# Seven-product form for every 512-cubed product of a two-layer graph network, and layer 1's weights as row dot products

## The chip, the cores and the metric

The kernel runs on one core of one Trainium2 chip. The metric is the device time of one execution in microseconds (us), less is better. All runs quoted of one kernel agree within about 0.3%. TensorE multiplies matrices, VectorE, ScalarE and GpSimd work element by element, and each engine takes its instructions in one fixed order. In the profile they are PE (PEld is its weight load), DVE, ACT and POOL.

## The reference, cut to what matters

There are 32 independent batches of 512 nodes with 512 features, all in f32. LN is a LayerNorm without parameters.

```
h  = max(LN(x), 0)
x  = x + relu([h, (adj h) / deg] W^T)          # layer 0, deg = row sums of adj
h1 = max(LN(x), 0)
q, k = split(h1 Wqk);  v = h1 Wv               # layer 1
w  = scale * mask * rowsum(q * (adj (mask k)))
x  = x + softmax(w)[:, None] * v
```

Both kernels fold Wq Wk^T into one 512x512 matrix once, so k is never formed. Per batch six products of 512 cubed are left.

## The kernel before

Each product is taken in four row chunks of 128. A chunk adds four matmuls of a 128x128 stationary block and 512 columns in one bank of PSUM:

```python
def product(p, pairs):
    for i, (lhsT, rhs) in enumerate(pairs):
        nc.tensor.matmul(p, lhsT, rhs, start=(i == 0), stop=(i == len(pairs) - 1))
```

LayerNorm's scaling runs on VectorE, and its relu is taken when ScalarE copies the transposed chunk out of PSUM. Layer 1's weights come from the full 512x512 matrix of q times h1, multiplied by the masked adj while its rows are summed. Four buffers each of x and adj let the loads run far ahead.

```python
def transpose_block(dst, src, c, func, name):
    p = ps_t.tile([P, 4, P], F32, tag="t", name=name)
    for d in range(4):
        nc.tensor.transpose(p[:, d, :], src[:, ts(d, P)], ident)
    nc.scalar.activation(dst[:, :, ts(c, P)], p, func)
# ... in layer1(b), after q^T = (h1 m)^T:
for c in range(C):
    p = mm_tile(f"ps_{b}_{c}")
    product(p, [(q[:, e, ts(c, P)], h1T[:, e, :]) for e in range(D)])
    nc.vector.scalar_tensor_tensor(
        am[:, c, :], p, mcol[:, c, b:b + 1], am[:, c, :],
        op0=ALU.mult, op1=ALU.mult, accum_out=w[:, c:c + 1])
# ...
for i in range(B + 1):   # layer 0 of batch i, layer 1 of i - 1, preparation of i + 1
    ...
```

The source gives a program order. The framework's scheduler turns it, by durations that it estimates, into one fixed instruction order for each engine; a later instruction is put ahead where an earlier one is thought not to be ready.

Of the kernel before, what the change touches and what calls it, by code (L numbers as in the profile page):

```python
# [15 lines left out]
P = 128  # L16
DEG_EPS = 1e-6
# [4 lines left out]
def kernel(  # L22
# [10 lines left out]
    """Layer 0: x1 = x + relu([h | adj h / deg] W^T), h = relu(LN(x)).  # L33
    Layer 1: out = x1 + softmax_i(w) * (h1 Wv), h1 = relu(LN(x1)), with
    w_i = scale m_i sum_j adj_ij m_j (q_i . k_j) and q_i . k_j = h1_i (Wq Wk^T) h1_j.

    Both layers use h only with the features on the partitions, so LN's result is
    transposed and the relu is taken on the way out of PSUM. adj / deg goes through
    the transpose already scaled, so that both halves of layer 0 add up in one
    PSUM bank as h W1^T + (adj / deg) (h W2^T).  # L40
    """
    nc = tc.nc
# [8 lines left out]
    small = ctx.enter_context(tc.tile_pool(name="small", bufs=4))  # L51
    ps_t = ctx.enter_context(tc.tile_pool(name="ps_t", bufs=2, space=bass.MemoryType.PSUM))
    ps_m = ctx.enter_context(tc.tile_pool(name="ps_m", bufs=5, space=bass.MemoryType.PSUM))
    ps_s = ctx.enter_context(tc.tile_pool(name="ps_s", bufs=1, space=bass.MemoryType.PSUM))

    def tile4(tag, bufs, name):
        return big.tile([P, 4, 512], F32, tag=tag, bufs=bufs, name=name)

    X, A, MB = {}, {}, {}

    def load(b):
        X[b] = tile4("x", 4, f"x_{b}")
        nc.sync.dma_start(out=X[b], in_=x[b].rearrange("(c p) f -> p c f", p=P))
        A[b] = tile4("adj", 4, f"adj_{b}")
        nc.sync.dma_start(out=A[b], in_=adj[b].rearrange("(c p) j -> p c j", p=P))
        MB[b] = small.tile([P, N], F32, tag="mb", name=f"mb_{b}")
        nc.sync.dma_start(out=MB[b], in_=nodemask[b].partition_broadcast(P))

    def transpose_block(dst, src, c, func, name):
        """dst[:, d, block c] = func(src[:, d-th block]^T) for the 4 blocks d of src [P, 512]."""  # L70
        p = ps_t.tile([P, 4, P], F32, tag="t", name=name)
        for d in range(4):
            nc.tensor.transpose(p[:, d, :], src[:, ts(d, P)], ident)  # L73
        nc.scalar.activation(dst[:, :, ts(c, P)], p, func)  # L74

    def product(p, pairs):
        for i, (lhsT, rhs) in enumerate(pairs):
            nc.tensor.matmul(p, lhsT, rhs, start=(i == 0), stop=(i == len(pairs) - 1))  # L78

    def mm_tile(name):  # L80
        return ps_m.tile([P, 512], F32, tag="m", name=name)

# [9 lines left out]
    wv_sb = const.tile([P, D, F], F32, name="wv_sb")  # L92
    mask_sb = const.tile([B, N], F32, name="mask_sb")
    w_in = []
    for half, tag in ((w0[:, 0:F], "x"), (w0[:, F:2 * F], "x"), (wqk[:, 0:F], "adj"), (wqk[:, F:2 * F], "adj")):
        t = tile4(tag, 4, f"w_in{len(w_in)}")
        nc.sync.dma_start(out=t, in_=half.rearrange("(c p) f -> p c f", p=P))
        w_in.append(t)
    nc.sync.dma_start(out=wv_sb, in_=wv.rearrange("(c p) f -> p c f", p=P))
    nc.sync.dma_start(out=mask_sb, in_=nodemask)  # L100
    load(1)

    w1T = const.tile([P, D, F], F32, name="w1T")
    w2T = const.tile([P, D, F], F32, name="w2T")
    wqT = tile4("q", 1, "wqT")
    wkT = tile4("h1T", 1, "wkT")
    m_sb = const.tile([P, D, F], F32, name="m_sb")

    XN, HT, AT = {}, {}, {}

    def layer_norm(b, name):
        """(x - mean) / sqrt(var + eps) of X[b], row chunk by row chunk."""
        mv = small.tile([P, C, 2], F32, tag="mv", name=f"mv{name}")
        rstd = small.tile([P, C], F32, tag="rstd", name=f"rstd{name}")
        for c in range(C):
            st = small.tile([P, 6], F32, tag="st", name=f"st{name}_{c}")
            nc.vector.bn_stats(st, X[b][:, c, :])  # L117
            nc.vector.bn_aggr(mv[:, c, :], st)
        nc.vector.tensor_scalar(rstd, mv[:, :, 1], LN_EPS, None, op0=ALU.add)  # L119
        nc.gpsimd.tensor_tensor(rstd, rstd, mhalf, op=ALU.pow)  # L120
        xn = tile4("xn", 2, f"xn{name}")
        for c in range(C):
            nc.vector.tensor_scalar(  # L123
                xn[:, c, :], X[b][:, c, :], mv[:, c, 0:1], rstd[:, c:c + 1],
                op0=ALU.subtract, op1=ALU.mult,
            )
        return xn

    def prepare(b):
        xn = layer_norm(b, f"0_{b}")  # L130
        rdeg = small.tile([P, C], F32, tag="rdeg", name=f"rdeg_{b}")
        nc.vector.tensor_reduce(rdeg, A[b], AX.X, ALU.add)
        nc.vector.tensor_scalar(rdeg, rdeg, DEG_EPS, None, op0=ALU.max)
        nc.vector.reciprocal(rdeg, rdeg)
        an = tile4("an", 1, f"an_{b}")
        for c in range(C):
            nc.vector.tensor_scalar(an[:, c, :], A[b][:, c, :], rdeg[:, c:c + 1], None, op0=ALU.mult)  # L137
        HT[b] = tile4("hT", 2, f"hT_{b}")
        for c in range(C):
            transpose_block(HT[b], xn[:, c, :], c, AF.Relu, f"pth_{b}_{c}")  # L140
        AT[b] = tile4("aT", 2, f"aT_{b}")
        for c in range(C):
            transpose_block(AT[b], an[:, c, :], c, AF.Copy, f"pta_{b}_{c}")
        mb = MB.pop(b)
        for c in range(C):
            nc.gpsimd.tensor_tensor(A[b][:, c, :], A[b][:, c, :], mb, op=ALU.mult)  # L146

    def layer0_y(b):
        y = tile4("y", 1, f"y_{b}")
        for c in range(C):  # L150
            p = mm_tile(f"py_{b}_{c}")
            product(p, [(HT[b][:, d, ts(c, P)], w2T[:, d, :]) for d in range(D)])
            nc.scalar.activation(y[:, c, :], p, AF.Copy)  # L153
        return y

    def layer0_out(b, y):
        hT, aT = HT.pop(b), AT.pop(b)
        for c in range(C):
            p = mm_tile(f"po_{b}_{c}")
            product(  # L160
                p,
                [(hT[:, d, ts(c, P)], w1T[:, d, :]) for d in range(D)]
                + [(aT[:, j, ts(c, P)], y[:, j, :]) for j in range(C)],
            )
            nc.vector.scalar_tensor_tensor(  # L165
                X[b][:, c, :], p, 0.0, X[b][:, c, :], op0=ALU.max, op1=ALU.add
            )
        XN[b] = layer_norm(b, f"1_{b}")

    def layer1_h(b):  # L170
        h1T = tile4("h1T", 1, f"h1T_{b}")
        xn = XN.pop(b)
        for c in range(C):
            transpose_block(h1T, xn[:, c, :], c, AF.Relu, f"pt1_{b}_{c}")
        return h1T

    def layer1(b, h1T):
        q = tile4("q", 1, f"q_{b}")
        for e in range(D):
            p = mm_tile(f"pq_{b}_{e}")  # L180
            product(p, [(m_sb[:, d, ts(e, P)], h1T[:, d, :]) for d in range(D)])
            nc.scalar.activation(q[:, e, :], p, AF.Copy)  # L182

        pv = {}

        def v_chunk(c):
            pv[c] = mm_tile(f"pv_{b}_{c}")
            product(pv[c], [(h1T[:, d, ts(c, P)], wv_sb[:, d, :]) for d in range(D)])

        v_chunk(0)  # L190
        am = A.pop(b)
        w = small.tile([P, C], F32, tag="w", name=f"w_{b}")
        for c in range(C):
            p = mm_tile(f"ps_{b}_{c}")
            product(p, [(q[:, e, ts(c, P)], h1T[:, e, :]) for e in range(D)])
            nc.vector.scalar_tensor_tensor(  # L196
                am[:, c, :], p, mcol[:, c, b:b + 1], am[:, c, :],
                op0=ALU.mult, op1=ALU.mult, accum_out=w[:, c:c + 1],
            )
        top = small.tile([P, 1], F32, tag="top", name=f"top_{b}")  # L200
        nc.vector.tensor_reduce(top, w, AX.X, ALU.max)
        v_chunk(1)
        ptop = ps_s.tile([1, P], F32, tag="s", name=f"ptop_{b}")
# [3 lines left out]
        v_chunk(2)  # L207
        pbc = ps_s.tile([P, 1], F32, tag="s", name=f"pbc_{b}")
# [7 lines left out]
        v_chunk(3)  # L216
        psum = ps_s.tile([P, 1], F32, tag="s", name=f"psum_{b}")
# [3 lines left out]
        sm = small.tile([P, C], F32, tag="sm", name=f"sm_{b}")  # L221
        nc.vector.tensor_scalar(sm, e, rs, None, op0=ALU.mult)
        xo = X.pop(b)
        for c in range(C):
            nc.vector.scalar_tensor_tensor(
                xo[:, c, :], pv[c], sm[:, c:c + 1], xo[:, c, :], op0=ALU.mult, op1=ALU.add
            )
        nc.sync.dma_start(out=out[b].rearrange("(c p) f -> p c f", p=P), in_=xo)

# [1 line left out]
    prepare(0)  # L231
    for t, dst in zip(w_in, (w1T, w2T, wqT, wkT)):
        for c in range(4):
            transpose_block(dst, t[:, c, :], c, AF.Copy, f"ptw_{dst.name}_{c}")
    for d in range(D):
        p = mm_tile(f"pm_{d}")
        product(p, [(wqT[:, a, ts(d, P)], wkT[:, a, :]) for a in range(D)])
# [47 lines left out]
```

## Time and profile before

| | before |
|---|---|
| median of the runs | 2885.6 us |
| span of the profiled run | 2883.9 us |
| TensorE busy | 2860 us, 99% |
| next busiest engine | VectorE, 29% |
| one batch, steady | 88.45 us |

TensorE's busy share is an upper view of its work, because matmul records overlap. The distance from one matmul's start to the next one's is the better measure. The prediction below shows these lines.

### The profile page before, as it was taken

The numbers are of one execution on the slowest core, as the hardware profiler recorded it, in microseconds if no ns is written. First come the engines' busy times: TensorE is split into PE (matmuls) and PEld (weight loads), VectorE is DVE, ScalarE is ACT, GpSimd is POOL, SyncE is SP. The second block draws the span as 40 slices with busy tenths as digits, with TensorE's granted clock in tenths as the row PEclk, the third lists the DMA queues.
The fourth block names the chain that finished last, engine by engine and source line by source line (L and its number), as shares of the span: only waits on it lengthen the run. The fifth ranks groups of instructions, "written<-read, shape, count | busy, mean of one in ns | idle before, by whom it ended". The sixth has DMA issues, their size and how long they took to land.

```text
span 2883.9 us, 19045 instructions
## 1 busy us (share of the span) xinstructions
PE 2860.2 (99%) x7940; PEld 1356.2 (47%) x7940; DVE 837.3 (29%) x1762; ACT 381.5 (13%) x694; POOL 240.6 (8%) x198
## 2 busy tenths in 40 slices
PE   8999999999999999999999999999999999999998
PEld 4444444444444444444444444444444444444443
DVE  4323323233232232232332323322323323232111
ACT  3111011111011110111100111101111011111000
POOL 2101011010010110110100101101001011010000
PEclk9999999999999999999999999999999999999999
DMA  5011001110011110011100111100111001110000
GB/s 216 4 48 48 15 33 48 48 48 30 29 36 47 48 48 15 33 48 48 47 30 19 48 48 47 46 17 33 48 48 48 15 29 44 44 44 15 0 15 29
DMA packets 58070, 115.58 MB, mean 40 GB/s; under 512 B 2144, under 2 KB 2144, under 8 KB 57984
## 3 DMA queue, kind: packets, MB, share of 16 engines
q1 hardware_dynamic: 57984, 114.37, 11.4%
q8 instruction: 62, 1.02, 0.1%
q14 instruction: 24, 0.20, 0.0%
HBM read 80.81 MB, written 33.55 MB: 40 GB/s over the span
## 4 chain that ended last, share of the span: by engine, by line
PE 99%; DVE 1%; DMA 0%; issue 0%; POOL 0%; ACT 0%; DVEq 0%; POOLq 0%; ACTq 0%
PE po L78 30%; PE pv L78 15%; PE pq L78 15%; PE ps L78 15%; PE py L78 15%; PE pth L73 2%; PE pt L73 2%; PE pta L73 2%; PE pm L78 0%; PE pbc L209 0%; DMA x<-in_x_dram 0%; DVE st L117 0%; DVE an L137 0%; PE psum L218 0%; PE ptop L204 0%
## 5 line engine op out<-in xcount | busy, mean ns | idle before, releaser
L78 PE MATMUL po<-w1T,hT 128*128 128x512 f32 x1024 | 465.5, 592 | 0.0
L78 PE MATMUL pv<-wv_sb,h1T 128*128 128x512 f32 x1024 | 462.0, 595 | 0.0
L78 PE MATMUL py<-w2T,hT 128*128 128x512 f32 x1024 | 460.6, 593 | 0.0
L78 PE MATMUL po<-y,aT 128*128 128x512 f32 x1024 | 460.3, 592 | 0.0
L78 PE MATMUL pq<-h1T,m_sb 128*128 128x512 f32 x1024 | 444.8, 592 | 0.7 <-ACT h1T L74 0.7
L78 PE MATMUL ps<-h1T,q 128*128 128x512 f32 x1024 | 444.7, 592 | 0.0
L165 DVE SCALAR_TENSOR_TENSOR x<-po,x 128x512 f32<-128x512 f32 x128 | 88.5, 692 | 1014.9 <-PE po L78 1014.9
L78 PEld LDWEIGHTS pq<-h1T,m_sb 128*128 128x128 f32 x1024 | 194.5, 190 | 245.4 <-issue 237.5
L78 PEld LDWEIGHTS po<-y,aT 128*128 128x128 f32 x1024 | 194.6, 190 | 244.9 <-issue 244.9
L78 PEld LDWEIGHTS ps<-h1T,q 128*128 128x128 f32 x1024 | 194.6, 190 | 244.9 <-issue 244.9
L78 PEld LDWEIGHTS pv<-wv_sb,h1T 128*128 128x128 f32 x1024 | 189.4, 190 | 225.8 <-issue 225.3
L78 PEld LDWEIGHTS po<-w1T,hT 128*128 128x128 f32 x1024 | 189.7, 190 | 215.2 <-issue 215.2
L196 DVE SCALAR_TENSOR_TENSOR adj<-ps,mcol,adj 128x512 f32<-128x512 f32 x128 | 96.1, 751 | 615.2 <-PE ps L78 615.2
L146 POOL TENSOR_TENSOR adj<-adj,mb 128x512 f32<-128x512 f32 x128 | 175.4, 1399 | 1164.8 <-DVE an L137 1164.8
L78 PEld LDWEIGHTS py<-w2T,hT 128*128 128x128 f32 x1024 | 184.7, 190 | 184.6 <-issue 184.4
L182 ACT ACTIVATE q<-pq 128x512 f32<-128x512 f32 x128 | 76.4, 597 | 1187.3 <-PE pq L78 1187.3
L120 POOL TENSOR_TENSOR rstd<-rstd,mhalf 128x4 f32<-128x4 f32 x64 | 64.5, 1008 | 1385.2 <-DVE rstd L119 1385.2
L117 DVE BATCH_NORM_STATS2 st<-x 128x6 f32<-128x512 f32 x256 | 171.2, 680 | 18.1 <-DMA x<-in_x_dram 13.8
L137 DVE TENSOR_SCALAR an<-adj,rdeg 128x512 f32<-128x512 f32 x128 | 118.3, 986 | 95.2 <-PE pta L73 95.0
L123 DVE TENSOR_SCALAR xn<-x,mv,rstd 128x512 f32<-128x512 f32 x256 | 122.6, 543 | 54.0 <-POOL rstd L120 54.0
L153 ACT ACTIVATE y<-py 128x512 f32<-128x512 f32 x128 | 76.5, 598 | 312.9 <-PE py L78 312.9
L214 ACT ACTIVATE e<-w,nbc 128x4 f32<-128x4 f32 x32 | 9.5, 298 | 800.2 <-DVE nbc L211 800.2
(55 smaller groups left out, 974.4 us busy)
## 6 DMA issues: line engine op xcount, KB each, us to landing
x<-in_x_dram SPq DMA_DIRECT2D x32, 1024.0 KB, 5.2
adj<-in_adj_dram SPq DMA_DIRECT2D x32, 1024.0 KB, 5.3
out_dram<-x SPq DMA_DIRECT2D x32, 1024.0 KB, 4.3
mb<-in_nodemask_dram SPq DMA_DIRECT2D x32, 256.0 KB, 3.2
w_in<-in_L_gnn_W_dram SPq DMA_DIRECT2D x2, 1024.0 KB, 11.9
w_in<-in_L_gnn_Wqk_dram SPq DMA_DIRECT2D x2, 1024.0 KB, 15.1
wv_sb<-in_L_gnn_Wv_dram SPq DMA_DIRECT2D x1, 1024.0 KB, 15.6
mask_sb<-in_nodemask_dram SPq DMA_DIRECT2D x1, 64.0 KB, 12.5
```

The source lines that it names most:

```text
L73: nc.tensor.transpose(p[:, d, :], src[:, ts(d, P)], ident)
L78: nc.tensor.matmul(p, lhsT, rhs, start=(i == 0), stop=(i == len(pairs) - 1))
L117: nc.vector.bn_stats(st, X[b][:, c, :])
L120: nc.gpsimd.tensor_tensor(rstd, rstd, mhalf, op=ALU.pow)
L123: nc.vector.tensor_scalar(xn[:, c, :], X[b][:, c, :], mv[:, c, 0:1], rstd[:, c:c + 1], op0=ALU.subtract, op1=ALU.mult,)
L137: nc.vector.tensor_scalar(an[:, c, :], A[b][:, c, :], rdeg[:, c:c + 1], None, op0=ALU.mult)
L146: nc.gpsimd.tensor_tensor(A[b][:, c, :], A[b][:, c, :], mb, op=ALU.mult)
L153: nc.scalar.activation(y[:, c, :], p, AF.Copy)
L165: nc.vector.scalar_tensor_tensor(X[b][:, c, :], p, 0.0, X[b][:, c, :], op0=ALU.max, op1=ALU.add)
L182: nc.scalar.activation(q[:, e, :], p, AF.Copy)
L196: nc.vector.scalar_tensor_tensor(am[:, c, :], p, mcol[:, c, b:b + 1], am[:, c, :], op0=ALU.mult, op1=ALU.mult, accum_out=w[:, c:c + 1],)
L214: nc.scalar.activation(e, w, AF.Exp, bias=nbc)
```

## The change

The intent is to do less on TensorE. A product is split into 2x2 blocks of 256, and seven products of blocks replace eight (Strassen's idea, in Winograd's form with fewer sums). The sums of operand blocks are taken by VectorE and GpSimd, and the blocks of the result are put together by VectorE from banks and ScalarE's copies of banks. To make operands serve twice, layer 1's weights become row dot products of q with (adj/deg)(mask h1), multiplied by deg afterwards, so that the transposed adj of layer 0 is used again. The room for the sums is found by cutting x from four buffers to three and adj from four to one. LayerNorm with its relu becomes one ScalarE operation. The core of the diff, cut:

```diff
+    def left_sums(eng, t):
+        eng.tensor_tensor(t[:, S1], t[:, S3], t[:, A22], op=ALU.add)
+        eng.tensor_tensor(t[:, S2], t[:, S1], t[:, A11], op=ALU.subtract)
+        eng.tensor_tensor(t[:, S3], t[:, A11], t[:, S3], op=ALU.subtract)
+        eng.tensor_tensor(t[:, S4], t[:, A12], t[:, S2], op=ALU.subtract)
...
+    def product(name, pairs, c21, rest):
+        a, b, c = bank(f"a{name}"), bank(f"b{name}"), bank(f"c{name}")
+        r1, u2, u3 = tmp(f"r1{name}"), tmp(f"u2{name}"), tmp(f"u3{name}")
+        times(a, 1, pairs, True)
+        nc.scalar.activation(r1, a, AF.Copy)
+        times(c, 2, pairs, True)
+        rest(0, 0, c, r1)
+        times(a, 6, pairs, False)
+        nc.scalar.activation(u2, a, AF.Copy)
+        times(b, 5, pairs, True)
+        times(a, 7, pairs, False)
+        nc.scalar.activation(u3, a, AF.Copy)
+        rest(1, 1, b, u3)
+        times(a, 4, pairs, False)
+        c21(a)
+        times(b, 3, pairs, False)
+        rest(0, 1, b, u2)
...
-        X[b] = tile4("x", 4, f"x_{b}")
+        X[b] = tile4(big, "x", 3, f"x_{b}")
-        A[b] = tile4("adj", 4, f"adj_{b}")
+        A[b] = tile4(big, "adj", 1, f"adj_{b}")
...
+            nc.scalar.activation(dst(c), X[b][:, c, :], AF.Relu, bias=nb[:, c:c + 1], scale=rstd[:, c:c + 1])
...
-    for i in range(B + 1):
+    for i in range(B):
+        layer0_out(i)
+        if i > 0:
+            layer1_out(i - 1)
+        if i + 1 < B:
+            prepare(i + 1)
+            layer0_y(i + 1)
+        layer1_h(i)
+        layer1_w(i)
         if i + 2 < B:
             load(i + 2)
+    layer1_out(B - 1)
```

`times(p, k, ...)` is block product k (P1 to P7): four matmuls of 256 columns, twice that for the two pairs of z. The five product calls of a batch are y, z, q, g (adj h1) and v; their banks are ay, by, cy and so on. rest(...) is VectorE's addition of a bank and a temporary.

## The prediction

> **What bounds the kernel now.** I read the page first: busy shares, then the chain that ended last, then the costliest groups.
>
> ```profile
> PE 2860.2 (99%) x7940; PEld 1356.2 (47%) x7940; DVE 837.3 (29%) x1762; ACT 381.5 (13%) x694; POOL 240.6 (8%) x198
> ...
> PE 99%; DVE 1%; DMA 0%; issue 0%; POOL 0%; ACT 0%; DVEq 0%; POOLq 0%; ACTq 0%
> ```
>
> TensorE is busy for 99% of the span and is 99% of the chain that ended last, so both views name the same bound. The next busiest engine has 29%. A busy TensorE need not be at its peak, so I went to the order of its instructions in a steady batch (the timeline) for the true spacing:
>
> ```profile
> 1329.75 0.25 PE L218 MATMUL psum<-es,ones 128*128 128x1 f32 x1
> 1329.87 1.07 PE L73 MATMUL pth<-ident,xn 128*128 128x128 f32 x8
> 1330.78 1.02 PE L78 MATMUL py<-w2T,hT 128*128 128x512 f32 x2
> 1331.64 1.04 PE L73 MATMUL pth<-ident,xn 128*128 128x128 f32 x8
> ...
> 1366.06 3.60 PE L78 MATMUL po<-y,aT 128*128 128x512 f32 x8
> 1369.49 3.60 PE L78 MATMUL po<-w1T,hT 128*128 128x512 f32 x8
> 1372.92 3.60 PE L78 MATMUL po<-y,aT 128*128 128x512 f32 x8
> 1376.36 13.90 PE L78 MATMUL pq<-h1T,m_sb 128*128 128x512 f32 x32
> 1390.09 3.60 PE L78 MATMUL pv<-wv_sb,h1T 128*128 128x512 f32 x8
> ```
>
> Columns are start, length, engine, line, operation, out<-in, count, in us. Three readings. First, a product of 512 cubed shows 32 instructions, not the 16 of the source: each f32 matmul is two, which start every (1390.09-1376.36)/32 = 0.429 us. Second, a transpose costs (1330.78-1329.87)/8 = 0.11 us. Third, the source emits all transposes of the next batch before the first py, but the trace has py between the two pth groups: the scheduler of the framework fills TensorE's waits with later work that is ready. The same pth group returns at 1418.31, so a batch takes 88.44 us; 32 batches are 2830 us, and 2883.9-2830 = 54 us is start and end. The windows view gives clock 1.00 for a batch. So time falls only if TensorE's own work falls, and stays fallen only if no new waits appear.
>
> **What the skill says.** (1) "TensorE: Matmul & The Clock Gate", Back-to-back issue gap: the isolated warm gap is about N/2.4 + 2.5 ns. With two cycles a column for each f32 half, 512 columns give 426.7+2.5 = 429.2 and 128 columns 106.7+2.5 = 109.2. The trace agrees with both (429 and about 109), so for 256 columns, which no instruction here has, I take the line through both: 215.8 ns. The same section also states about 131 ns for N=512 in a sustained stream; this f32 trace doesn't show that. (2) The same page, Step-by-step, says the next weights load while this matmul runs. The trace shows a load of 190 ns in each 429 ns; at 216 ns it must fit with little slack. (3) "VectorE: DVE Perf Modes", The perf-mode tier table: f32 tensor_tensor has only the 1x rate. The trace's two-input operation on 512 elements takes 692 ns. (4) "PSUM — Partial Sum Buffer", PSUM bank collisions: reader and TensorE must not be in one bank together. That matters for the product that accumulates in a bank that was just copied.
>
> **The change, part by part.**
> *TensorE.* Six products of 512 cubed per batch before (py, po twice, pq, ps, pv) and six after (y, z twice, q, adj h1, v). Each had 32 instructions of 512 columns, 13.73 us; each now has 7 x 4 matmuls x 2 = 56 of 256 columns, 56 x 0.2158 = 12.08 us. That is 7/8 of the columns (0.875), and 0.88 of the time with the 2.5 ns. Six give 82.4 before and 72.5 after. The 48 transposes stay: 5.2 us. The softmax's little matmuls and the rest of the 88.44 are 0.8 us. After: 72.5+5.2+0.8 = 78.5 us a batch, 9.9 less; over 32 batches 2513 us.
> *Start and end.* Before 54 us. After, the weight sums are added (VectorE and GpSimd, mostly beside the 13.7 us of Wq Wk^T), the first z has no earlier batch to fill with, and the last h1 transposes must wait until the v of the batch before has let go of the single h1T buffer, some 3 us. I put 60 us (estimate).
> *VectorE.* Slope from the reduce (2048 elements, 2285 ns) and the 692 ns: about 1.04 ns an element and 0.16 us fixed. Per batch: 8 left sums and 15 additions of a bank to a temporary at 0.69 = 15.9; 4 finishes of z at 0.69 = 2.8; 8 halves of v at 0.48 = 3.8; 8 row dots with accumulator at about 0.51 = 4.1; LayerNorm statistics 8 x (0.68+0.17) = 6.8; the adj reduce 2.3; small ones 2.5. Sum 38 us of 78.5, 49% (26 now). It is not the bound.
> *ScalarE.* 17 bank copies and 12 transpose copies at 0.6 = 17.4; 8 LayerNorm relus at about 0.72 and 4 adj scalings at about 0.7 = 8.6; exp 0.3: 26 us, 33% (11.5 now).
> *GpSimd.* 12 sums at the 1.40 us of its adj<-adj,mb row, 4 maskings at no more, 2 powers at 1.0: at most 24 us, 31%.
> *New waits.* In each product call bank a is filled by P1, P6, P7 and P4 in turn and copied between. After P7 both P4 (bank a, being copied) and P3 (bank b, whose reader needs that copy) must wait. What such a hop costs is seen at the end of the run:
>
> ```profile
> 2830.73 1.09 ACT L74 ACTIVATE h1T<-pt 128x512 f32<-128x512 f32 x2 [3.81 <-PE pt L73]
> 2831.38 0.91 PEld L73 LDWEIGHTS pt<-ident,xn 128*128 128x128 f32 x8 [0.55 <-ACT h1T L74]
> 2831.38 1.15 PE L73 MATMUL pt<-ident,xn 128*128 128x128 f32 x8 [0.31 <-ACT h1T L74]
> ...
> 2832.08 1.08 ACT L74 ACTIVATE h1T<-pt 128x512 f32<-128x512 f32 x2 [0.26 <-PE pt L73]
> ...
> 2833.22 1.12 PE L78 MATMUL pq<-h1T,m_sb 128*128 128x512 f32 x2 [0.69 <-ACT h1T L74]
> ```
>
> The first four transposes of the second group end about 2831.82 and ScalarE starts at 2832.08, 0.26 later; a copy lasts 0.6; TensorE follows its end (2833.16) by 0.06. A hole of about 0.9 us, five product calls a batch: 4.5 us if nothing fills it. Two f32 matmuls of the next product (0.86 us) fill it, and six banks allow two products in flight. The neighbours seem ready: v after z, y's transposes in v, h1's transposes in y, adj h1 after q, the next z after adj h1. The other copies have a whole P (1.7 us) of cover. The softmax chain (no v chunks between its three little matmuls any more) has the next z as filler. The operand sums of hT (4 x 0.69 = 2.8 us) lie behind P1 and P2 (3.4 us), which need none of them, as waits here follow parts of a tile: statistics of one x chunk start at 1370.42, before the last chunk is written at 1376.56. I leave 1.3 us of waits a batch, 42 us, for what the static order gets wrong (a choice, between 0 and 4.5).
> *Sum.* 2513 + 60 + 42 = 2615 us.
>
> **The rivals.**
> (a) *The hand-over holes stay open*: 32 x 4.5 = 144 instead of 42 gives 2717. For: each product now goes to and fro with ScalarE and VectorE seven times in 12 us, in a fixed order chosen from estimated durations. Against: py stands inside the pth groups, and TensorE waits 14 us in the whole run now.
> (b) *Weight loads become the bound.* The load shows 190 ns, and 216 leaves 26. If a pair took 240 ns, a batch were 336 x 0.24+6 = 86.6 and the run about 2830. Against: transposes run every 109 ns with a load each, and the one-column pair pbc takes 0.31 us for two loads and two matmuls, so a load needs no more than some 0.15 us.
> (c) *Operand sums come late.* After y, GpSimd has y's sums (5.6), then masking and sums of h1 (up to 11.2): 17 us, while q lasts 12. Product adj h1 would then wait, but its P1 and P2 don't need the last sums and the next z can fill. If it costs 4 us a batch: 2740.
> (d) *VectorE or ScalarE becomes the bound.* 49% and 33% by the sums above; they would have to double. I give it almost nothing.
>
> **Range and chances.** Nothing unforeseen and all holes filled gives 2573, so the lower end is 2555, with some room for the start. Rival (a) whole gives 2717, so the upper end is 2725. A result within 2% needs over 2828 us, that is 255 us of waits, 8 us a batch: rival (b) or (a) and (c) together. Faster 0.94, same 0.04, slower 0.02.
>
> **What would show it.** Instructions of 256 columns at 216 ns start to start, 1792 to a product and over 12,000 on TensorE; its clock 1.00; a batch of 79 to 81 us. Right also: at P7's end other tiles' matmuls stand before P4. Wrong: TensorE idle of 0.9 us named after ScalarE's bank copies (a), PEld busy near 90% with a spacing over 216 (b), idle named after GpSimd's sums (c), TensorE's share of the chain under 90%, or a batch over 84 us.

## The result, and the profile after

The changed kernel takes 2676.4 us (median of 4 runs, 2676.3 to 2679.6) against 2885.6 for the kernel before in the same rounds. The ratio is 0.928, with a 95% interval of 0.926 to 0.929. Ratios here are the mean time of one kernel's fast runs over that of the other's of the same rounds, so not quite the ratio of the medians quoted. A steady batch takes 81.9 us on average.

The page of the changed kernel, in its first part (busy us, share, instructions) and its fourth (the chain that ended last, by engine):

```profile
PE 2588.8 (97%) x12548; PEld 2208.7 (82%) x12548; DVE 1182.8 (44%) x2666; ACT 804.0 (30%) x1375; POOL 790.0 (30%) x590
...
PE 72%; DVE 14%; DMA 6%; ACT 5%; POOL 2%; issue 1%; DVEq 0%
```

TensorE's busy share has fallen by two points only, but the chain that ends last now runs over TensorE for only 72% of the span. Before, the chain was TensorE almost alone (99%). Now it goes to and fro over the other engines' queues. What TensorE waited for is in the view of waits (total us, times, longest us):

```profile
PE av L115 <- ACT u3v L134: 42.8, 32, 1.4
PE aq L115 <- DVE h1T L76: 13.6, 20, 1.0
...
PE by L115 <- DVE y L144: 6.1, 7, 3.9
```

The first of these comes once in every batch. Here it is in TensorE's timeline of one batch, with q's wait of the same batch:

```profile
1313.23 1.89 PE L115 MATMUL av<-wvv,h1T 128*128 128x256 f32 x8
1314.96 1.04 PE L98 MATMUL pth<-ident,h 128*128 128x128 f32 x8
1317.39 1.99 PE L115 MATMUL av<-wvv,h1T 128*128 128x256 f32 x8 [1.39 <-ACT u3v L134]
...
1340.24 1.89 PE L115 MATMUL cq<-wm,h1T 128*128 128x256 f32 x8
1342.89 1.97 PE L115 MATMUL aq<-wm,h1T 128*128 128x256 f32 x8 [0.76 <-DVE h1T L76]
```

P7 of v starts at 1313.23, and its eight instructions take (1314.96-1313.23)/8 = 0.216 us each. Eight transposes of the next batch follow (0.87 us), and then P4 of v waits for the copy of bank a. ScalarE's timeline in the same stretch says why:

```profile
1314.63 2.22 ACT L188 ACTIVATE h<-x,nb,rstd 128x512 f32<-128x512 f32 x3 [2.32 <-DVE nb L186]
1316.76 0.57 ACT L134 ACTIVATE u3v<-av 128x512 f32<-128x512 f32 x1
```

Three LayerNorm relus stand in ScalarE's queue before the copy u3v. They got their input late (they had waited 2.32 us for VectorE's nb) and took 2.22 us, so the copy began 1.8 us after P7's last slot (1314.96) instead of the 0.26 that the prediction had read for such a hop.

To see the small losses too, I took each start-to-start distance on TensorE less the instruction's own spacing (0.109, 0.216 or 0.429 us) and summed what exceeds 15 ns over the steady batches; the softmax's one-column matmuls have no spacing taken off. The kernel before loses 0.67 us a batch this way, around the softmax's small matmuls. The changed kernel loses 3.95: v's hole 1.55, q's before P6 0.52 and inside its matmuls 0.16, y's 0.2 and 0.09, the softmax as before, and the rest in tenths at hand-overs.

Elsewhere the holes are filled, as the prediction had it. This is P7 of z, P1 of v, P4 of z:

```profile
1381.23 1.03 PE L115 MATMUL az<-y,aT 128*128 128x256 f32 x4
1382.10 1.03 PE L115 MATMUL av<-wvv,h1T 128*128 128x256 f32 x4
1382.96 1.12 PE L115 MATMUL az<-w,hT 128*128 128x256 f32 x4
```

### The profile page after: what moved, and what is told of

Same layout as the page of the kernel before. It is cut to its first block, busy times and chain, and to the rows that moved or that the text cites. A ratio compares the mean times of both kernels' runs of the same rounds, so it can differ in the third digit from the quotient of the medians.

```text
span 2677.8 us, 30643 instructions
## 1 busy us (share of the span) xinstructions
PE 2588.8 (97%) x12548; PEld 2208.7 (82%) x12548; DVE 1182.8 (44%) x2666; ACT 804.0 (30%) x1375; POOL 790.0 (30%) x590
## 4 chain that ended last, share of the span: by engine, by line
PE 72%; DVE 14%; DMA 6%; ACT 5%; POOL 2%; issue 1%; DVEq 0%
PE az L115 17%; PE ag L115 9%; PE bz L115 8%; PE aq L115 7%; DVE st L182 5%; PE cz L115 4%; PE bg L115 4%; PE bq L115 4%; DMA adj<-in_adj_dram 4%; PE av L115 4%; PE ay L115 3%; ACT h L188 3%; PE bv L115 2%; POOL rstd L185 2%; PE cg L115 2%; PE pta L98 2%
## 5 line engine op out<-in xcount | busy, mean ns | idle before, releaser
L115 PE MATMUL av<-wvv,h1T 128*128 128x256 f32 x1024 | 250.7, 382 | 42.8 <-ACT u3v L134 42.8
L115 PE MATMUL az<-w,hT 128*128 128x256 f32 x1024 | 265.7, 382 | 0.3 <-ACT u3z L134 0.3
L115 PE MATMUL aq<-wm,h1T 128*128 128x256 f32 x1024 | 252.4, 384 | 13.6 <-DVE h1T L76 13.6
L115 PE MATMUL az<-y,aT 128*128 128x256 f32 x1024 | 262.8, 379 | 0.0
L115 PE MATMUL ay<-w,hT 128*128 128x256 f32 x1024 | 256.1, 383 | 2.5 <-ACT u3y L134 1.5
L115 PE MATMUL ag<-h,aT 128*128 128x256 f32 x1024 | 249.5, 381 | 0.0
L247 POOL TENSOR_SCALAR h<-h,mraw 128x512 f32<-128x512 f32 x128 | 214.8, 1684 | 86.7 <-PE pt L98 86.7
L188 ACT ACTIVATE h<-x,nb,rstd 128x512 f32<-128x512 f32 x256 | 196.7, 806 | 97.7 <-DVE nb L186 90.2
L115 PEld LDWEIGHTS ag<-h,aT 128*128 128x128 f32 x1024 | 191.9, 190 | 35.8 <-issue 11.0
L115 PEld LDWEIGHTS az<-y,aT 128*128 128x128 f32 x1024 | 194.6, 190 | 26.5
```

Source lines behind the costliest of these rows:

```text
L115: nc.tensor.matmul(p[:, m, :], left[:, LEFT[k], kt, ts(m, P)], right[:, RIGHT[k], kt, :], start=(start and m == 0 and i == 0), stop=(i == ...
L188: nc.scalar.activation(dst(c), X[b][:, c, :], AF.Relu, bias=nb[:, c:c + 1], scale=rstd[:, c:c + 1])
L247: nc.gpsimd.tensor_scalar(rows(c), rows(c), mraw[:, c, b:b + 1], None, op0=ALU.mult)
```

## The experiments

The theory after the first look: TensorE has less to do, as reckoned, and what it lost again lies in single hand-overs, where work for another batch stands before the needed copy or sum in a strictly ordered queue. The rivals: the hand-over itself is too long and nothing can fill it; the added sums make VectorE late; or the rewrite around the products, not the products, moves the time. All twelve kernels gave correct results. The times:

| run | what differs | us | ratio to before |
|---|---|---|---|
| (the change) | | 2676.4 | 0.928 |
| e1_plain | the change without the seven products | 2992.2 | 1.037 |
| e2_u3v_vector | v's u3 copied by VectorE | 2633.6 | 0.913 |
| e3_p3_in_c | P3 in bank c, before P4 | 3028.3 | 1.049 |
| e4_norm_vector | LayerNorm's scaling on VectorE | 2679.0 | 0.928 |
| e5_p3_in_c_root_vector | e3, root on VectorE | 2755.2 | 0.955 |
| e6_u3v_adj2 | e2, h0 in q's buffer, two adj | 2621.9 | 0.909 |
| e7_all | P3 in c, e4, root, h0 in q's buffer, two adj | 2727.5 | 0.945 |
| e8_plain_buffers | e1 with the old x and adj buffers | 2933.4 | 1.017 |
| e9_u3v_h0q | e2, h0 in q's buffer, one adj | 2615.1 | 0.906 |
| e10_norm_adj2 | e4, h0 in q's buffer, two adj | 2615.2 | 0.906 |
| e11_norm_u3v_h0q | e2 and e4 together, h0 in q's buffer | 2648.0 | 0.917 |
| e12_row_dots_alone | the kernel before with row dots only | 2891.0 | 1.002 |

### e1_plain: the rewrite without the seven products

```diff
-        times(a, 1, pairs, True)   # ... seven block products, sums before, additions after
+        for c in range(4):
+            half, m = divmod(c, 2)
+            p = bank(f"p{name}_{c}")
+            # for left, right in pairs, kh and kt in range(2):
+            nc.tensor.matmul(p, left[:, 2 * half + kh, kt, ts(m, P)],
+                             right[:, 2 * kh:2 * kh + 2, kt, :], start=..., stop=...)
+            rest(c, p)
```

> The changed kernel with ordinary products on the same operand layout: eight blocks, 512 columns, no sums; the row dots, the LayerNorm on ScalarE and the single adj buffer stay. Theory A (the gain is the count of TensorE columns, the rest of the rewrite neither gives nor takes): 192 x 0.4292 + 48 x 0.109 + 0.8 = 88.4 us a batch, 32 of them and about 57 us of start and end, so 2886 us, within 1% of the kernel before, TensorE 99% busy. Rival (the rewrite itself moves the time, by fewer VectorE operations on adj or by LayerNorm waits): outside 2850 to 2920.

It took 2992 us, 106 more than the kernel before, outside what both theories said. So the rest of the rewrite, with plain products, is not neutral. Within this rewrite the seven products are worth 2992-2676 = 316 us. That is what the prediction's 32 x 9.9 = 317 us says of TensorE's columns, but the agreement is partly luck, because the two kernels wait for different things: here TensorE waits 65.9 us for h1T's copies and VectorE 313 us for x, in the changed kernel 1.1 and 6.9 us. So the 106 us of e1 are not a cost that the changed kernel bears as well. Where the 106 us went is in TensorE's timeline:

```profile
1300.77 1.04 PE L92 MATMUL pt<-ident,h 128*128 128x128 f32 x8
1303.90 0.84 PE L92 MATMUL pt<-ident,h 128*128 128x128 f32 x4 [2.09 <-ACT h1T L94]
1304.53 1.92 PE L112 MATMUL pq<-wm,h1T 128*128 128x512 f32 x2
1306.24 1.06 PE L92 MATMUL pt<-ident,h 128*128 128x128 f32 x4
```

The transposes of h1 wait for ScalarE, whose queue holds relus and adj scalings of a later batch first. Then the two matmuls after the hole take (1306.24-1304.53)/2 = 0.855 us each, twice the 0.429: the hole also cost the clock, which the view of windows gives as 0.50 from 1304.3 to 1307.6. (The run's clock record has such a stretch of 3.41 us 15 times in 32 batches.) The Trainium skill, "TensorE: Matmul & The Clock Gate", Part 4, says that the full clock doesn't engage for transposes, which don't count as busy, and its Part 1 that an idle window of about 3.4 us drops the clock to half. This trace agrees: from the last product matmul to the first pq are some 3.8 us with nothing but 12 transposes. VectorE had stood waiting for loads, as the view of its waits over the whole run of e1_plain shows (us in total, number of waits, longest in us): 313 us in 31 waits, about 10 us a batch.

```profile
DVE st L157 <- DMA x<-in_x_dram: 313.0, 31, 16.7
```

### e8_plain_buffers: is it the buffers that the sums displaced?

```diff
-        return pool.tile([P, 7, 2, H], F32, tag=tag, bufs=bufs, name=name)
+        return pool.tile([P, 4, 2, H], F32, tag=tag, bufs=bufs, name=name)
-        X[b] = tile4(big, "x", 3, f"x_{b}")
+        X[b] = tile4(big, "x", 4, f"x_{b}")
-        A[b] = tile4(big, "adj", 1, f"adj_{b}")
+        A[b] = tile4(big, "adj", 4, f"adj_{b}")
```

> e1_plain with the buffers of the kernel before again: operands of four blocks instead of seven, four x and four adj buffers. Theory J (e1's 106 us over the kernel before come from the buffers that Strassen's sums displaced: x and adj land late and their LayerNorm and scaling stand in ScalarE's queue ahead of h1T's copies): within 1% of the kernel before, 2860 to 2915. Rival K (the move of LayerNorm's relu to ScalarE, or the row dots, costs it): above 2950, with TensorE waiting for h1T copies as in e1.

It took 2933 us, between the two ranges. The wait for x loads falls from 313 to 18 us, the batch falls from 92.4 to 90.0 us, and 59 of the 106 us come back. So theory J holds for a good half. The remaining 48 us are 1.6 us a batch, in small gaps between groups of transposes and before the softmax; which part of the rewrite makes them was not taken apart further. Not all buffers are the old ones here: hT keeps one where the kernel before has two, and the program order and LayerNorm's relu on ScalarE stay new; each of these is an untested candidate.

### e12_row_dots_alone: the second half of the change by itself

```diff
-            product(p, [(m_sb[:, d, ts(e, P)], h1T[:, d, :]) for d in range(D)])
+            product(p, [(h1T[:, d, ts(e, P)], m_sb[:, d, :]) for d in range(D)])
...
-            product(p, [(q[:, e, ts(c, P)], h1T[:, e, :]) for e in range(D)])
+            product(p, [(aT[:, j, ts(c, P)], h1m[:, j, :]) for j in range(C)])
+            g = small.tile([P, 512], F32, tag="g", name=f"g_{b}_{c}")
             nc.vector.scalar_tensor_tensor(
-                am[:, c, :], p, mcol[:, c, b:b + 1], am[:, c, :],
-                op0=ALU.mult, op1=ALU.mult, accum_out=w[:, c:c + 1],
+                g, p, 1.0, q[:, c, :], op0=ALU.mult, op1=ALU.mult, accum_out=w[:, c:c + 1],
             )
```

(GpSimd masks h1 instead of adj; adj has three buffers, the transposed adj and the normalised x three; w is multiplied by deg and mask afterwards.)

> The kernel before with only the second part of the change: layer 1's weights as row dot products of q with (adj/deg)(mask h1), ordinary products of 512 columns, LayerNorm as before, GpSimd masking h1 instead of adj, three adj buffers, three aT. TensorE has the same 192 and 48 instructions a batch. Theory L (row dots give no time by themselves): within 0.5% of the kernel before, 2872 to 2900. Rival K (the row dots cost part of e8's 48 us): 2905 or more.

It took 2891 us, 0.2% more than before: theory L. Row dots give nothing by themselves. They make room and let an operand's sums be used twice.

### e2_u3v_vector: one copy moved to the other queue

```diff
-        nc.scalar.activation(u3, a, AF.Copy)
+        if u3_on_vector:          # in the product v only
+            nc.vector.tensor_copy(u3, a)
+        else:
+            nc.scalar.activation(u3, a, AF.Copy)
```

> In the product v alone VectorE instead of ScalarE copies bank a to u3. Theory B (the 1.55 us hole before v's P4 is the copy standing in ScalarE's queue behind three LayerNorm relus): the copy starts some 0.2 us after P7, lasts 0.7, and the eight transposes (0.87) cover nearly all of it; 32 x 1.35 = 43 us less, 2633 us, and the wait of av for u3v falls from 43 us to under 10. Rival C (the hole is the hand-over itself, whoever copies, because nothing else is ready): 2665 to 2680, the same wait now named after VectorE.

It took 2633.6 us, where theory B said 2633. The wait of av, 42.8 us before, is in the waits of this run:

```profile
PE av L115 <- DVE u3v L135: 0.9, 1, 0.9
```

The copy is even longer than before (0.69 us on VectorE, 0.57 on ScalarE). A comparison of the two traces shows that TensorE's 12548 instructions and GpSimd's come in the same order to the last one, VectorE's differ by the 32 copies alone, and on ScalarE one relu a batch moves up into the copy's old place. So the 1.55 us was the place in the queue, not the hand-over (rival C falls for v).

### e3_p3_in_c: more cover for the copy

```diff
         times(b, 5, pairs, True)
+        nc.vector.tensor_tensor(u2, b, u2, op=ALU.add)
         times(a, 7, pairs, False)
         nc.scalar.activation(u3, a, AF.Copy)
         rest(1, 1, b, u3)
+        times(c, 3, pairs, True)
+        rest(0, 1, c, u2)
         times(a, 4, pairs, False)
         c21(a)
-        times(b, 3, pairs, False)
-        rest(0, 1, b, u2)
```

> P3 goes into bank c, free by then, between P7 and P4, and b is added to u2 by one more VectorE operation (5 x 0.69 us a batch): every copy of u3 gets 1.73 us of cover. Theory D (holes at hand-overs are all that is left to take there): v's hole of 1.55, y's of 0.2 and the 0.1 at the others close, 32 x 1.85 = 59 us less, 2617 us. Rival E (the added VectorE work or the reuse of c delays the sums of hT and h1T and opens waits elsewhere): 2650 or more, with waits named after VectorE.

It took 3028 us, far worse than even rival E's lower end. On paper this closes every hole at P4, and it did close v's (0.5 us opened before v's P7 instead). But another order of instructions came out of it, and before q's P6 TensorE now stands for 11.6 us. VectorE, GpSimd and TensorE in that stretch:

```profile
1321.06 1.10 DVE L75 TENSOR_TENSOR h1T<-h1T 128x512 f32<-128x512 f32 x1 [1.31 <-ACT h1T L100]
1330.62 3.65 DVE L187 SCALAR_TENSOR_TENSOR nb<-mv,rstd 128x4 f32<-128x4 f32 x1 [8.46 <-POOL rstd L186]
1334.20 0.68 DVE L76 TENSOR_TENSOR h1T<-h1T 128x512 f32<-128x512 f32 x1
```

```profile
1328.01 1.57 POOL L248 TENSOR_SCALAR h<-h,mraw 128x512 f32<-128x512 f32 x1
1329.54 1.05 POOL L186 TENSOR_TENSOR rstd<-rstd,mhalf 128x4 f32<-128x4 f32 x1
1330.55 1.27 POOL L82 TENSOR_TENSOR h<-h 128x512 f32<-128x512 f32 x1
1331.77 1.27 POOL L83 TENSOR_TENSOR h<-h 128x512 f32<-128x512 f32 x1
1332.99 1.27 POOL L84 TENSOR_TENSOR h<-h 128x512 f32<-128x512 f32 x1
```

```profile
1335.03 3.32 PE L115 MATMUL aq<-wm,h1T 128*128 128x256 f32 x7 [11.61 <-DVE h1T L76]
```

The sum S2 (L76), which P6 needs, stands on VectorE behind nb, a tiny operation of a later batch's LayerNorm. nb waits 8.46 us for the power on GpSimd, which stands behind masks and operand sums. One queue blocks the next, which blocks the next. Order is not the whole of it: nb itself then takes 3.65 us, as long as GpSimd's three sums of h run beside it. With no GpSimd instruction beside it, nb takes 0.16 us (median of 33 in this run). So some 3.5 of the 11.6 us are an operation made slow, not one in the wrong place. TensorE's seven matmuls after the hole run at half rate, too (granted clock 0.50 from 1335.0 to 1338.3).

### e5_p3_in_c_root_vector: cutting that chain

```diff
-        nc.vector.tensor_scalar(rstd, mv[:, :, 1], LN_EPS, None, op0=ALU.add)
-        nc.gpsimd.tensor_tensor(rstd, rstd, mhalf, op=ALU.pow)
+        nc.vector.tensor_scalar(v2, mv[:, :, 1], 0.5, 0.5 * LN_EPS, op0=ALU.mult, op1=ALU.add)
+        nc.vector.tensor_scalar(rstd, v2, 0.5, None, op0=ALU.add)
+        for _ in range(3):
+            nc.vector.reciprocal(hq, rstd)
+            nc.vector.tensor_tensor(hq, hq, v2, op=ALU.mult)
+            nc.vector.scalar_tensor_tensor(rstd, rstd, 0.5, hq, op0=ALU.mult, op1=ALU.add)
+        nc.vector.reciprocal(rstd, rstd)
```

> P3 in bank c as in e3_p3_in_c, and LayerNorm's power -0.5 no longer goes to GpSimd: VectorE takes the root in some twelve small operations (0.17 us each). Theory F (e3's hole of 10.5 us before q's P6 is a chain of queues: the S2 sum of h1T stands on VectorE behind the next-but-one batch's LayerNorm, which waits for its power on GpSimd, which stands behind masks and sums): the hole falls under 1.5 us, 3028 becomes 2680 or less, 2620 if P3's cover then counts as I first reckoned. Rival G (P3 in c or the added VectorE operation itself makes the hole): above 2900.

It took 2755 us: 273 less than e3, so the chain over GpSimd, its wait and its slowing of nb together, was the main cause and rival G falls; but theory F's 2680 was missed. The hole before q's P6 fell from 10.5 us on average to 2.9, not below 1.5, because the cure stands in the same place:

```profile
1293.78 1.19 DVE L188 TENSOR_SCALAR rstd<-v 128x4 f32<-128x4 f32 x1
...
1298.53 0.66 DVE L75 TENSOR_TENSOR h1T<-h1T 128x512 f32<-128x512 f32 x1
```

From 1293.78 to 1298.53 the root's small operations for a later batch run before h1T's first sum, some of them at 1.1 us instead of 0.17; the long ones are again those with GpSimd work beside them.

### e4_norm_vector: taking the relus out of ScalarE's queue

```diff
-            nc.scalar.activation(dst(c), X[b][:, c, :], AF.Relu, bias=nb[:, c:c + 1], scale=rstd[:, c:c + 1])
+            nc.vector.tensor_scalar(dst(c), X[b][:, c, :], mv[:, c, 0:1], rstd[:, c:c + 1],
+                                    op0=ALU.subtract, op1=ALU.mult)
...
-        nc.scalar.activation(dst[...], p, AF.Copy)      # transposes of h and h1
+        nc.scalar.activation(dst[...], p, AF.Relu)
-            nc.gpsimd.tensor_scalar(rows(c), rows(c), mraw[:, c, b:b + 1], None, op0=ALU.mult)
+            nc.gpsimd.tensor_scalar(rows(c), rows(c), 0.0, mraw[:, c, b:b + 1], op0=ALU.max, op1=ALU.mult)
```

> LayerNorm's scaling goes back to VectorE (0.543 us each in the kernel before), the relu into ScalarE's copy of the transposes and into GpSimd's masking: eight relus of 0.8 us a batch leave ScalarE's queue. Theory B (relus in ScalarE's queue make both the hole before v's P4 and that before q's P6): v's 1.55 falls to about 0.1 and q's 0.68 to about 0.2, 32 x 1.9 = 61 us less, 2615 us. Rival C leaves v's hole (2660 or more); rival E (VectorE, with 4.3 us more a batch, gets late itself) makes q's hole larger: 2640 or more.

It took 2679 us, no change, and both theories were right in part. v's hole fell from 1.55 to 0.2 us, as B said. q's before P6 grew from 0.52 to 1.96, as E said. VectorE's timeline before q's P6 (which waits for L76):

```profile
1341.62 3.06 DVE L186 TENSOR_SCALAR h<-x,mv,rstd 128x512 f32<-128x512 f32 x4 [0.56 <-POOL rstd L184]
1344.61 0.68 DVE L75 TENSOR_TENSOR h1T<-h1T 128x512 f32<-128x512 f32 x1
1345.32 0.69 DVE L76 TENSOR_TENSOR h1T<-h1T 128x512 f32<-128x512 f32 x1
```

Four scalings for the batch after next run there for 3.06 us, as soon as that batch's x has landed, and the urgent sums stand behind them.

### e10_norm_adj2, e6_u3v_adj2, e9_u3v_h0q: keeping the early work out of the way

What may run early is set by when its output buffer is free. h0, the normalised x, had a buffer of its own, free right after the transposes. If it shares q's, it cannot be written until q has been used:

```diff
-        h0 = tile4(big, "h0", 1, f"h0_{b}")
+        h0 = tile4(big, "q", 1, f"h0_{b}")
-        A[b] = tile4(big, "adj", 1, f"adj_{b}")
+        A[b] = tile4(big, "adj", 2, f"adj_{b}")      # e6 and e10; e9 keeps one
```

(The raw Wq, which had used q's buffer, is loaded into an adj buffer. e6 and e9 have e2's copy on VectorE, e10 has e4's LayerNorm.)

> e4_norm_vector (LayerNorm's scaling on VectorE, u3 copies all on ScalarE) with h0 in q's buffer and two adj buffers. Theory H: e4 closed v's hole (1.55 to 0.2 us) and lost it again before q's P6 (0.7 to 2.2) because four scalings for the next-but-one batch, 3.1 us, stood on VectorE before h1T's sums; with h0 in q's buffer they can't, q's hole falls under 0.3, 2679 becomes 2612. Rival: VectorE is late for other reasons (statistics, reduction), 2655 or more.

It took 2615 us, as theory H said (2612). TensorE's waits for u3v and for h1T's sums (0.7 and 55.6 us in e4) have shrunk to one each, and the batch is 79.8 us:

```profile
PE av L115 <- ACT u3v L134: 0.7, 1, 0.7
...
PE aq L115 <- DVE h1T L76: 0.2, 1, 0.2
```

VectorE's timeline has no scaling before h1T's sums any more. So e4's gain had been real and had been eaten by the early scalings.

> e2_u3v_vector with a second adj buffer, paid for by giving h0 the buffer of q (so the next-but-one batch's LayerNorm cannot write before adj h1 is done). Theory H (the holes left before q's P6, 0.47+0.16 us, and before y's P3 come from work on the x and adj that land just then, standing ahead of the hand-over's own work): they close, 32 x 0.7 = 22 us less than e2's 2634, 2611 us. Rival I (they are the hand-over's own length): 2634 within 8 us. If h0's later start opens a hole before y instead, more than 2645.

It took 2622 us, between H's 2611 and I's 2634. q's hole is closed (0.09 us is left in its matmuls), but a gap of 0.27 us appeared before the softmax's transpose.

> e6_u3v_adj2 with one adj buffer again: v's u3 on VectorE, h0 in q's buffer, nothing else. If h0's later start is what closed q's hole (the next-but-one batch's LayerNorm relus can't stand before h1T's copies), 2622 as e6. If the second adj buffer did it (adj lands earlier, its reduction and scaling leave the queue), 2634 as e2.

It took 2615 us, below both numbers: h0's buffer did it. The second adj buffer, which I had held for half of the cure, gave nothing; with it the kernel is 7 us slower, as the 0.27 us before the softmax in e6 would make it. One steady batch of this run in the view of windows (length, then busy us of each engine, granted clock, DMA share, GB/s):

```profile
1320.00:1399.66 79.66, 79.63 (x391) 68.71 (x390) 36.16 (x84) 24.31 (x41) 24.18 (x19) 1.00 0.12 40
```

The reckoned floor for TensorE was 78.5 us. e9 and e10 are both 2.3% faster than the changed kernel and 9.4% faster than the kernel before.

### e7_all and e11_norm_u3v_h0q: all cures together

e7 is the sum of the diffs of e3, e4 and e5 and h0 in q's buffer with two adj buffers; e11 is the sum of e2, e4 and h0 in q's buffer with one adj.

> All cures together: P3 in c, LayerNorm's scaling and root on VectorE, relu in the transposes' copies, second adj buffer with h0 in q's. Theories B, F and H together leave some 0.8 us of waits a batch: 32 x 79.3 + 57 = 2595 us. If VectorE (about 38+3.5+4.3+4.8 = 51 us of 79 a batch) becomes late in its queue: 2640 or more.

e7 took 2727 us, the second branch of the expectation. The root's small operations stand before h1T's sums again, and q's hole is about 3 us. ScalarE's copies were there in time; VectorE's sums were not.

> The two cures that worked, together, with one adj buffer: v's u3 copied by VectorE, LayerNorm's scaling on VectorE with the relu in the transposes' copies and in GpSimd's mask, h0 in q's buffer. The cures overlap (both take relus out of the way of v's u3), so little is left: if the holes of 0.2 us at v and y shrink, 2605 to 2612; if they only move, 2615 as e9 and e10.

e11 took 2648 us, worse than e9 and e10, which have one of the two cures each; I had not thought of that. e2 works because the copy leaves the queue that holds LayerNorm; e4 works because LayerNorm leaves the queue that holds the copy. Done together, both stand on VectorE, and v's hole is back with 1.16 us:

```profile
1299.66 1.91 DVE L189 TENSOR_SCALAR h<-x,mv,rstd 128x512 f32<-128x512 f32 x4 [1.14 <-POOL rstd L187]
1301.49 0.68 DVE L135 COPY u3v<-av 128x512 f32<-128x512 f32 x1
```

```profile
1302.23 1.99 PE L115 MATMUL av<-wvv,h1T 128*128 128x256 f32 x8 [0.99 <-DVE u3v L135]
```

This is the strongest support of the queue theory: the same picture on another engine.

## Why the prediction was right or wrong

- **The range held.** 2676 us lies in 2555 to 2725, and the kernel is faster by 7%. The point, 2615, was 61 us too low. Of its own signs, the spacing, the clock and other tiles' matmuls before P4 came true. The batch of 79 to 81 us did not (81.9), and two of its signs of being wrong came true: TensorE's share of the chain under 90% (72%), and TensorE idle named after a bank copy (1.39 us before v's P4). Its sums hold; one slip is TensorE's 14 us of waits before, which add up to 14.9.
- **TensorE's work was right.** 256 columns start every 0.216 us, and the clock in a steady batch is 1.00. Rival (b) falls: PEld is busy 82%, a load still shows 190 ns, and it hides behind 216.
- **Start and end were right.** 2677.8 less 32 batches of 81.92 leaves 56 us, against 60; its parts were not checked one by one.
- **The loads of the other engines were right.** 36.5, 24.7 and 24.3 us in one batch for VectorE, ScalarE and GpSimd, against 38, 26 and at most 24. Only the masking was mis-sized: 1.68 us each, not under 1.40.
- **The term that was mis-sized is the new waits, "1.3 us of waits a batch".** TensorE's losses are 3.95 us, of which 0.67 were there before, so 3.3 us are new. The excess of 2.0 us a batch is 64 us and explains the miss of 61.
- **Why it was mis-sized.** The prediction looked at whether TensorE had other work to fill a hole, and at the length of a copy (0.9 us with the hand-over). It took the copy to start 0.26 us after the matmuls. In v the eight transposes did fill 0.87 us, but the copy started 1.8 us after P7, behind relus. e2 shows this as cause: 43 of the 61 us. (Point (4) of the prediction, on PSUM banks, no run was made to test.) The holes at q went when the later batch's relus were held off ScalarE (e9, 18 us more): h1T's copies, which VectorE's sums for q wait for, had stood behind them. e9's batch, 79.7 us, is then the predicted 79.8; that the 1.3 us fits it is luck, for it was a choice. Busy shares of 30% hid it: the queue was not full, only in the wrong order.
- **Rival (a) held in part**: of five holes one stayed open. **Rival (c)** named sums that come late before adj h1; that did not occur, but h1T's sums came late before q, on VectorE, which waits 45.0 us in all for ScalarE's h1T copies there (17.6 in e9). **Rival (d)** falls as a bound, yet VectorE's order decided e3, e4, e5, e7 and e11.
- **Not foreseen at all:** with plain products the rewrite around them costs time by itself (e1, 106 us; more than half from the buffers, by e8). The prediction had counted the smaller buffers only at the end of the run. These waits are not part of the miss of 61 us, since the changed kernel hardly has them (see e1). Nor did it foresee that VectorE's operand sums last longer beside GpSimd's: S2 of h1T took 0.98 us before the q hole shown above, where 0.69 was reckoned.

What stays open: the source of e8's remaining 48 us, why the last tenths at hand-overs stay, and what the slowing of VectorE beside GpSimd costs in all; no run took it away by itself.

## What to carry to other kernels

When TensorE's work is cut and the other engines take it over, the sum of busy times tells which engine could be the bound, but the waits come from the order within each queue: find, for every hand-over that TensorE waits for, what stands before it in that queue, above all work for a later batch that became possible just then. Such work can be held off by the buffer that it writes to, which cost nothing here and was worth more than a second load buffer. Two cures that each move one of two colliding things can restore the collision when both are done.

## What the Trainium skill lacked or had wrong

- "TensorE: Matmul & The Clock Gate" gives no spacing for f32 products. Here each f32 matmul is two instructions, and they start every 429 ns at 512 columns and 216 ns at 256; f32 transposes of 128 columns start every 109 ns. That is its isolated formula with two cycles a column. Its 131 ns for 512 columns in a sustained stream is not seen in any run, all of them f32. (Passes of FP32 are counted elsewhere in the skill, without a time.)
- The same page gives a weight load as its columns over 1.2 (107 ns for 128). Loads of f32 product weights show 190 ns in every kernel here, and the loads for transposes 141 to 148 ns; neither was the bound. As the latter start every 109 ns, a load's record is longer than what it keeps busy, so these records don't refute the page's figure.
- "GPSIMD Engine Reference" calls one-input operations roughly line-rate (Engine selection). GpSimd's mask, one input with a per-partition factor, took 1.68 us in the mean for 512 elements (1.57 in e1, where GpSimd takes no sums), more than most of its two-input sums (1.27 us).
- The same page says that GpSimd shares its SBUF interfaces with VectorE, and gives no size there; the skill treats this sharing elsewhere too, so only the size here is new. The same sum of 512 elements took VectorE, in the groups of the changed kernel:

```profile
L78 DVE TENSOR_TENSOR h1T<-h1T 128x512 f32<-128x512 f32 x32 | 56.1, 1753 | 0.0
...
L78 DVE TENSOR_TENSOR hT<-hT 128x512 f32<-128x512 f32 x32 | 23.0, 718 | 0.0
```

  The first, 1753 ns in the mean, runs beside GpSimd's sums, the second does not. Over all sums of hT and h1T in this trace the median is 686 ns with no GpSimd instruction beside them (126 sums) and 1752 ns beside a two-input sum of GpSimd (39); VectorE's additions of a PSUM bank keep 692 ns in both cases (300 and 129). So the overlap decides it; that is read from one trace, and no run tested it by itself.
- No page that I used says what a fixed instruction order costs when operations become ready in another order than it has them: 1.55 us a batch in the changed kernel, most of the 10.5 us in e3.
